# Four dense layers with paged attention on one core: six weight loads dropped, 64 small subtractions moved from VectorE to GpSimd

## The chip, the core and the metric

The kernel runs on one core of one Trainium2 chip. The core has TensorE (PE) for matrix products, VectorE (DVE), ScalarE (ACT) and GpSimd (POOL) for everything else, and SyncE (SP), which here only issues transfers; 16 DMA engines move data between the device memory and the on-chip memory. The engines run their own instruction streams, each strictly in order, and meet through semaphores. The metric is the device time of one execution in microseconds; the kernel is run several times and the median is taken. Separately one execution is recorded by the hardware profiler; times inside the kernel come from that one.

## The reference

An input `x` of 64 sequences of 32 rows with 512 features (2048 rows) goes through four residual layers, `x = x + ffn(cond(x))`:

- Layer 0: one of 8 weight matrices per sequence, then a two-matrix ReLU² network plus a routed low-rank part, and a layer norm.
- Layer 1: a gated network (512 to 1376 and back) with a low-rank update per sequence, then a 512x512 product with a thresholded mixture of low-rank experts.
- Layer 2: paged attention, 32 query heads over 8 key and value heads of width 128, against 512 cached keys per sequence (16 pages of 32 rows, named by a table of indices) and the 32 new rows, with a norm and a rotation on queries and keys, and an output product by `Wo` (4096 to 512); then a 512x512 product with 2 of 8 low-rank experts.
- Layer 3: one of 32 small mixing matrices per sequence, a 512x512 product, and low-rank updates.

All of it is float32.

## The kernel before

The 2048 rows are 16 tiles of 128 rows (`NT`), each of four sequences. The layers run one after the other; layer 3 and the dense part of layer 2 form a common tail.

**Layer 1** (`layer1`) takes two tiles at a time: 8 groups of 256 rows. For a group, `features(f)` for f = 0 to 10 forms the gate and up products for one chunk of 128 of the 1376 features; each ends in two DVE instructions (L426, L427) that write a slice of `actT`. `down` then accumulates the product with the down weights in four blocks `pz`. Its last part (chunk 10 and the low-rank term, L438) needs `low_d`, which `low_down` computes with small PE products and one DVE instruction (`masked`, L384). The main loop (L512) interleaves the groups: beside the products of group g come the choice of experts and the output of group g-1 and the loads for group g+1 (`load_updates`: the first halves `A` of the low-rank updates by SP, and three gathers `Bg`, `Bu`, `Bd` by POOL; `load_x`: two tiles `xt`).

Layer 1 also prepares something for layer 2. The output product of layer 2 multiplies two-by-two blocks of matrices with 7 instead of 8 products, for which four sums of blocks of `Wo` are wanted. `sum_up` (L272) makes three steps for one block row: `rows` loads two pieces of 256 KB (L283, SP), `add` forms four differences of 128x256 (L289 to L292), `store` writes 512 KB to the device memory (L295, SP). There are 16 such sums, two per group. Loaded and computed tiles come from one ring of three buffers named `sum`, so the load for sum k+2 needs the buffer that the store of sum k reads. The tile framework orders instructions of independent work by priority, and it brings the sums forward: the program has nearly all 16 inside the first of the 8 groups, ahead of instructions of `low_d` on DVE.

**Layer 2** (`attention`) goes through 32 steps: two halves of the heads (`HALVES`), for each the 16 tiles. In step s, PE works on the scores and values of tile s, and between them, at fixed places called slots, on the projections of step s+1 (values, keys and four groups of query heads, with 4 matmuls of 512 columns per pair of places) and on the output product of earlier tiles. A step has 32 slots; which work stands at which slot is written out by hand (`plan`, `then`, `slots`, L1056 to L1121). Every projection weight tile (`wv`, `wk`, and four `wq`, 1 MB each) has one buffer, holding the weights of the current half. The weights of the second half are loaded over those of the first by this part:

```
if steps[s + 2][0] != h:
    for what, at in zip(("v", "k") + GROUPS, (4, 6, 9, 12, 15, 18)):
        slots[at].append(partial(weights, steps[s + 2][0], what))
```

Here `h` is the half of step s. The condition holds for s = 14 and for s = 15. In step 14 each load stands after the last use of the weights by the projections of step 15, which is the last of the first half. In step 15 the same six loads stand once more. An odd step's plan has the keys at slots 2 and 4, the query groups at 5 and 6, 8 and 9, 11 and 13, 19 and 20, and the values at 22 and 24, so the loads of step 15 come after the projections of step 16 for keys and query groups 0 to 2, and before those for query group 3 (load at slot 18) and for the values (load at slot 4).

SP issues all of these loads and also the page loads `kt` in one queue in program order.

Of the kernel before, what the change touches and what calls it, by code (L numbers as in the profile page):

```python
# [28 lines left out]
ALU = mybir.AluOpType  # L29
# [242 lines left out]
def sum_up(c, pool, sums, h, k):  # L272


    nc, a = c.nc, c.a
    H = D // 2
    w, t = [], []

    def rows():
        w.append(pool.tile([P, 4, H], F32, name="sum", bufs=3))  # L280
        for n in range(2):
            at = (h * HQP + n * HQP // 2 + k) * HD
            nc.sync.dma_start(w[0][:, 2 * n:2 * n + 2, :].rearrange("p a b -> p (a b)"),  # L283
                              a["WoT"][at:at + HD, :])

    def add():
        t.append(pool.tile([P, 4, H], F32, name="sum", bufs=3))
        (b11, b12, b21, b22), (t1, t2, t3, t4) = ([v[0][:, n, :] for n in range(4)] for v in (w, t))
        nc.vector.tensor_tensor(t1, b12, b11, ALU.subtract)  # L289
        nc.vector.tensor_tensor(t3, b22, b12, ALU.subtract)  # L290
        nc.vector.tensor_tensor(t2, b22, t1, ALU.subtract)
        nc.vector.tensor_tensor(t4, b21, t2, ALU.subtract)  # L292

    def store():
        nc.sync.dma_start(sums[h][:, k], t[0])  # L295

    return rows, add, store
# [340 lines left out]
def attention(c, known, x_in, y_part, y_out, sums, tail):  # L638
# [14 lines left out]
    tc, nc, a = c.tc, c.nc, c.a  # L653
    half = HD // 2
    n_c = L // P
    with ExitStack() as outer:
# [304 lines left out]
        steps = [(h, T) for h in range(HALVES) for T in range(NT)]  # L961
# [91 lines left out]
        for s, (h, T) in enumerate(steps):  # L1053
# [35 lines left out]
            if s + 2 < len(steps):  # L1089
                slots[18].append(projections[s + 2].load)  # L1090
                slots[24].append(projections[s + 2].tables)
                slots[29 if s < 2 else 26].append(projections[s + 2].x)
                if steps[s + 2][0] != h:

                    for what, at in zip(("v", "k") + GROUPS, (4, 6, 9, 12, 15, 18)):
                        slots[at].append(partial(weights, steps[s + 2][0], what))
# [268 lines left out]
def emit(tc, a, layers=(0, 1, 2)):  # L1365
    with ExitStack() as ctx:
        c = Common(ctx, tc, a)
        dram = ctx.enter_context(tc.tile_pool(name="scratch", bufs=1, space=DRAM))

        def scratch(name):  # L1370
            tiles = [dram.tile([P, D], F32, name=f"{name}_{t}") for t in range(NT)]
            return lambda t: tiles[t]

        def rows(name):
            return lambda t: a[name][t * P:(t + 1) * P, :]

        x = rows("x")
        for n in layers:
            out = rows("out") if n == layers[-1] else scratch(f"x{n}")
            if n == 0:  # L1380
                layer0(c, x, out)
            if n != 0 and n == next(m for m in layers if m):
                kp = ctx.enter_context(tc.tile_pool(name="known", bufs=1))
                last = Tail(c)
                last.numbers(kp)
                known = Known(c, kp)
                sums = [dram.tile([P, HQP // 2, 4, D // 2], F32, name=f"wo_sums{h}") for h in range(HALVES)]
            if n == 1:
                layer1(c, kp, x, out, sums)
            elif n == 2:  # L1390
                y_part, y = scratch("y_part"), scratch("y")
                attention(c, known, x, y_part, y, sums, last.between(x, y, out))
            x = out
# [86 lines left out]
```

## Time and profile before

| | |
|---|---|
| runs of the kernel | median 3666.28 us of 3 (3663.46 to 3667.42) |
| the profiled execution | 3653.76 us, of it 3652.0 us from first to last instruction (the span) |
| PE busy | 3589.3 us, 98% of the span |
| DVE, ACT, POOL busy | 1909.3, 1294.5, 1371.1 us |
| layer 1 in the trace | about 397 to 1071 us |
| layer 2's attention | about 1072 us to the tail |
| moved by DMA | 533.45 MB |

The span is the profiled execution's own stretch from its first to its last instruction; 1.8 us lie around it. "Idle before" of an instruction is the time in which its engine stood still ahead of it, with the event that ended the wait. Idle time of DVE, ACT or POOL costs nothing as long as PE doesn't wait for them.

### The profile page before, as it was taken

To read this page: it belongs to the slowest core of one execution; us is meant where nothing else is said; L and a number is where in the kernel's file an instruction comes from. 1 tells how busy PE (TensorE), PEld (TensorE's weight loads), DVE (VectorE), ACT (ScalarE), POOL (GpSimd) and SP (SyncE) were. 2 spreads that over 40 slices of the span, in tenths; PEclk is the share of its full clock that TensorE was granted. 3 is DMA by queue.
4 is the path that set the end of the run, shared out by engine and by line. 5 is a ranking of instruction groups with operands and counts; after the bars stand their busy time and mean duration, and the time that the engine had idled before them with its cause. 6 is when DMAs were issued, how large, how long until landed. Compare 5 with 4: busy or idle time off the path is not lost.

```text
span 3652.0 us, 60353 instructions
## 1 busy us (share of the span) xinstructions
PE 3589.3 (98%) x19520; PEld 2669.0 (73%) x19520; DVE 1909.3 (52%) x4996; ACT 1294.5 (35%) x3046; POOL 1371.1 (38%) x1343
## 2 busy tenths in 40 slices
PE   8999999999999999999999999999999999999999
PEld 3444778888867788777877877778777788777855
DVE  5453332222226756666666655566566665666533
ACT  1111111111115544444444444444444444444411
POOL 0112100000025644555445453455554544555232
PEclk9999999999999999999999999999999999999999
DMA  5004541110124555555655577555555565556731
GB/s 211 24 27 167 189 136 44 54 52 31 41 93 126 150 184 179 166 174 152 186 184 153 181 224 228 184 153 181 170 184 172 152 189 172 179 173 200 219 99 62
DMA packets 531083, 533.45 MB, mean 146 GB/s; under 512 B 54258, under 2 KB 441330, under 8 KB 530770
## 3 DMA queue, kind: packets, MB, share of 16 engines
q1 hardware_dynamic: 484050, 377.50, 33.4%
q0 software_dynamic: 44416, 147.88, 12.7%
q10 hardware_dynamic: 2304, 4.20, 0.3%
q8 instruction: 159, 2.61, 0.3%
q14 instruction: 154, 1.26, 0.1%
HBM read 500.01 MB, written 29.36 MB: 145 GB/s over the span
## 4 chain that ended last, share of the span: by engine, by line
PE 91%; DVE 4%; DMA 2%; SPq 1%; issue 1%; ACT 1%; POOL 0%; DVEq 0%; ACTq 0%; POOLq 0%
PE po L689 14%; PE sc L900 12%; PE pq L689 12%; PE gate_up L342 10%; PE py L689 9%; PE prT_ps L684 6%; PE pz L342 4%; PE po L1249 3%; PE pv L689 3%; PE pk L689 3%; PE ph L124 3%; PE pd L249 2%; DVE own_vt L722 2%; PE po L342 2%; PE qkT_ps L684 2%; PE py L204 1%
## 5 line engine op out<-in xcount | busy, mean ns | idle before, releaser
L715 POOL DMA_INDIRECT vt<-in_v_rows,v_rows x512 | 499.9, 976 | 592.1 <-PE po L689 486.7
L907 ACT ACTIVATE pr<-pr,low 128x544 f32<-128x544 f32 x512 | 383.4, 749 | 726.9 <-DVE low L905 723.5
L689 PEld LDWEIGHTS po<-prT,vt 128*128 128x128 f32 x4096 | 533.0, 192 | 96.8 <-issue 75.6
L900 PE MATMUL sc<-kt,qT 128*128 128x288 f32 (+1 forms) x2048 | 555.5, 394 | 4.4 <-ACT qT L803 2.4
L689 PE MATMUL po<-prT,vt 128*128 128x128 f32 x4096 | 542.4, 275 | 0.9 <-ACT prT L918 0.9
L905 DVE CUSTOM_DVE_ANT_0 pr<-sc,mask 128x544 f32<-128x544 f32 x512 | 368.8, 720 | 321.6 <-PE sc L900 320.1
L689 PE MATMUL pq<-wq,xT 128*128 128x512 f32 x1024 | 482.3, 594 | 8.3 <-DMA wq<-in_WqT 8.3
L900 PEld LDWEIGHTS sc<-kt,qT 128*128 128x128 f32 x2048 | 370.1, 190 | 154.4 <-issue 64.8
L918 ACT COPY prT<-prT_ps 128x512 f32<-128x512 f32 x512 | 296.0, 578 | 178.8 <-PE prT_ps L684 177.4
L912 DVE TENSOR_SCALAR pr<-pr,low 128x512 f32<-128x512 f32 x512 | 332.8, 650 | 15.2
L684 PE MATMUL prT_ps<-ident,pr 128*128 128x128 f32 x2048 | 311.2, 275 | 0.1
L689 PEld LDWEIGHTS pq<-wq,xT 128*128 128x128 f32 x1024 | 186.2, 191 | 141.7 <-issue 125.8
L909 DVE RECIPROCAL low<-low 128x1 f32<-128x1 f32 x512 | 83.2, 163 | 339.4 <-ACT pr L907 335.5
L684 PEld LDWEIGHTS prT_ps<-ident,pr 128*128 128x128 f32 x2048 | 238.2, 142 | 7.9 <-issue 0.3
L689 PE MATMUL py<-wo,oT 128*128 128x256 f32 x1024 | 241.4, 379 | 0.0
L128 POOL TENSOR_TENSOR rs<-rs,minus_half 128x4 f32<-128x4 f32 x160 | 169.1, 1057 | 160.3 <-DVE rs L731 156.1
L910 ACT ACTIVATE own_pr<-pr,low 128x32 f32<-128x32 f32 x512 | 164.0, 320 | 131.9 <-DVE low L909 130.6
L747 POOL TENSOR_TENSOR rot<-rot,swapped 128x512 f32<-128x512 f32 x160 | 204.9, 1280 | 5.2 <-DVE swapped L744 3.9
L689 PEld LDWEIGHTS py<-wo,oT 128*128 128x128 f32 x1024 | 187.5, 190 | 22.0
L722 DVE COPY own_vt<-v 32x128 f32<-32x128 f32 x512 | 171.6, 335 | 36.7 <-PE po L689 24.7
L689 PE MATMUL py<-wo,o_sum 128*128 128x256 f32 x768 | 181.5, 380 | 0.2
L730 DVE TENSOR_REDUCE rs<-squares 128x4 f32<-128x512 f32 x160 | 109.3, 683 | 136.2 <-ACT squares L728 134.5
(226 smaller groups left out, 5106.3 us busy)
## 6 DMA issues: line engine op xcount, KB each, us to landing
kt<-in_kT SPq DMA_DIRECT2D x2048, 64.0 KB
wo<-wo_sums SPq DMA_DIRECT2D x128, 512.0 KB
wo<-in_WoT SPq DMA_DIRECT2D x96, 512.0 KB
xt<-x SPq DMA_DIRECT2D x48, 256.0 KB
wq<-in_WqT SPq DMA_DIRECT2D x12, 1024.0 KB
A<-in_A SPq DMA_DIRECT2D x64, 152.0 KB
sets<-in_cond0T SPq DMA_DIRECT2D x32, 256.0 KB
sum<-in_WoT SPq DMA_DIRECT2D x32, 256.0 KB
```

The lines of the kernel that those rows point to most:

```text
L128: self.nc.gpsimd.tensor_tensor(t, t, self.minus_half[:, :n], ALU.pow)
L342: c.on_pe(nc.tensor.matmul(out, lhsT, rhs, start=start, stop=stop))
L684: c.on_pe(nc.tensor.transpose(pt[:, m, :], piece, c.ident))
L689: c.on_pe(nc.tensor.matmul(out, lhsT, rhs, start=first and i == 0, stop=last and i == len(pairs) - 1))
L715: nc.gpsimd.indirect_dma_start(out=vts[b % 2][:, n, :], out_offset=None, in_=a["v_rows"], in_offset=bass.IndirectOffsetOnAxis(ap=rows[h][: ...
L722: nc.vector.tensor_copy(own_vts[b % 2][g * S:(g + 1) * S, g % 2, :], v[j * S:(j + 1) * S, g * HD:(g + 1) * HD])
L747: nc.gpsimd.tensor_tensor(r, r, tmp, ALU.add)
L900: c.on_pe(nc.tensor.matmul(sc[:, lo + n * PSIZE:lo + m * PSIZE].rearrange("p (n k) -> p n k", k=PSIZE), q, kt[:, n:m, g, :], start=True, s ...
L905: nc.vector.tensor_tensor_reduce(pr[:, :NK], sc[:, lo:lo + NK], masks[h, b], -SCALE, 3.0e38, ALU.add, ALU.min, low[:, 0:1])
L907: nc.scalar.activation(pr[:, :NK], pr[:, :NK], AF.Exp, bias=low[:, 0:1], scale=-1.0, accum_out=low[:, 1:2])
L912: nc.vector.tensor_scalar(pr[:, :L], pr[:, :L], low[:, 2:3], None, ALU.mult)
L918: nc.scalar.copy(prT, pt)
```

## The change

Two edits that don't touch each other.

```
 def add():                                     # in sum_up
-    nc.vector.tensor_tensor(t1, b12, b11, ALU.subtract)
-    nc.vector.tensor_tensor(t3, b22, b12, ALU.subtract)
-    nc.vector.tensor_tensor(t2, b22, t1, ALU.subtract)
-    nc.vector.tensor_tensor(t4, b21, t2, ALU.subtract)
+    nc.gpsimd.tensor_tensor(t1, b12, b11, ALU.subtract)
+    nc.gpsimd.tensor_tensor(t3, b22, b12, ALU.subtract)
+    nc.gpsimd.tensor_tensor(t2, b22, t1, ALU.subtract)
+    nc.gpsimd.tensor_tensor(t4, b21, t2, ALU.subtract)
...
-    if steps[s + 2][0] != h:                   # in attention
+    if steps[s + 2][0] != steps[s + 1][0]:
         for what, at in zip(("v", "k") + GROUPS, (4, 6, 9, 12, 15, 18)):
             slots[at].append(partial(weights, steps[s + 2][0], what))
```

The first puts the 64 subtractions of layer 1 into POOL's stream. The second makes the condition true only for s = 14, where step s+2 is of another half than step s+1; the six loads of step 15 are no longer issued. The instructions of PE and ACT and their order stay as they were. DVE's order is the old one without the 64 subtractions. On SP the six loads of step 15 are gone, and in layer 1's first group some stores and loads of the sums change places with each other and with the loads of `A`.

## Prediction, made before the changed kernel was run

> **What bounds the kernel now.** I read the page's first part, then the waits of PE, then the two stretches around the two waits that touch the change. PE is busy for 98% of the span:
>
> ```profile
> PE 3589.3 (98%) x19520; PEld 2669.0 (73%) x19520; DVE 1909.3 (52%) x4996; ACT 1294.5 (35%) x3046; POOL 1371.1 (38%) x1343
> ```
>
> So only what PE waits for can be won: 3652.0 - 3589.3 = 62.7 us, the start of the program included. The list of PE's waits (total us, times, longest) has its largest entries here:
>
> ```profile
> PE py L204 <- DVE w L200: 12.1, 2, 11.0
> PE pq L689 <- DMA wq<-in_WqT: 8.3, 1, 8.3
> PE pz L342 <- DVE low_d L384: 6.7, 1, 6.7
> ```
>
> The first is layer 0's start, untouched. The second is one wait for a query weight load, the third one wait in layer 1. PE in time, first around the second entry:
>
> ```profile
> 2245.47 1.18 PE L900 MATMUL sc<-kt,qT 128*128 128x288 f32 x4
> 2255.00 3.57 PE L689 MATMUL pq<-wq,xT 128*128 128x512 f32 x4 [8.35 <-DMA wq<-in_WqT]
> 2258.40 0.60 PE L684 MATMUL qkT_ps<-ident,rot 128*128 128x128 f32 x4
> 2260.17 1.88 PE L689 MATMUL pq<-wq,xT 128*128 128x512 f32 x4
> ```
>
> Besides the 8.35 us of standing still, the four matmuls behind it take 3.57 us, and the same four 1.88 us a little later. SP's queue has the culprit, the last of the step's six repeated loads (start, duration of the issue):
>
> ```profile
> 2245.14 0.43 SPq L100 DMA_DIRECT2D wq<-in_WqT  x1
> ```
>
> Query group 3 is projected at slot 19 of step 15, its reload stands at slot 18, so PE waits for a megabyte that it already had.
>
> The third entry, on DVE in time:
>
> ```profile
> 469.93 0.43 DVE L292 TENSOR_TENSOR sum<-sum 128x256 f32<-128x256 f32 x1
> 474.66 0.43 DVE L289 TENSOR_TENSOR sum<-sum 128x256 f32<-128x256 f32 x1 [4.31 <-DMA sum<-in_WoT]
> 475.00 0.42 DVE L384 TENSOR_TENSOR low_d<-low_d_ps,own 128x256 f32<-128x256 f32 x1
> ```
>
> DVE stands 4.31 us before a subtraction whose block of `Wo` hasn't landed, with `low_d` queued behind it; its PE products were done at about 467.3. Then the same work of PE in group 0 and in group 1 (length, busy time per engine, granted clock, DMA), from the first matmul of `low_d_ps` to the first of the next group:
>
> ```profile
> 465.84:480.76 14.92, 8.25 (x169) 6.72 (x169) 9.23 (x20) 0.59 (x1) 0.00 (x0) 0.77 0.74 231
> 557.16:563.00 5.84, 5.84 (x169) 5.31 (x169) 3.15 (x4) 0.59 (x1) 0.00 (x0) 1.00 0.22 59
> ```
>
> The same 169 matmuls take 14.92 us with sums in DVE's queue and 5.84 us without.
>
> **What the Trainium skill says.** "TensorE: Matmul & The Clock Gate", What's actually happening: after an idle window of about 3.4 us the array runs at half its clock until it has been busy as long. The trace agrees: the clock of 0.77 above, and 3.57 against 1.88 us. "GPSIMD Engine Reference", Performance versus the Vector engine: an add of two float32 operands took 1.96 times as long as on VectorE. Here the nearest rows are POOL's additions of the same shape, L875 at 821 ns and L876 at 724 ns mean, against 424 ns for L289: 1.7 to 1.9. "SBUF — State Buffer", Who interferes with whom: a VectorE instruction with two inputs in SBUF, or a copy in a two-port mode, and a GpSimd instruction lock each other out for the length of one instruction; one with a single SBUF input doesn't contend. The trace agrees: one L292 took 1.43 us beside POOL's 1.27 us addition at 440.09, while L426, which has one PSUM input, took its 0.42 us beside another at 435.33.
>
> **Part 1, the weights.** Removed: six SP issues and 6 MB. From the start of the score matmuls at 2245.47 to the transposes at 2258.40 are 12.93 us. Undisturbed these are 0.92 (four `sc`) + 1.72 (four `pq`), as the chain of waits spaces them elsewhere: 2.64. Gain 12.93 - 2.64 = 10.3 us. What could be late next: nothing that PE waits for in step 13, which has the same plan and no loads (PE busy 75.95 of 76.00 us from 2035 to 2111). DVE was just in time for `sc` at 2245.47 (its L905 ended at 2245.41), so a few tenths may come back. The `xt` and page loads move forward. The first loading, in step 14, stays; PE stood nowhere in it (76.00 of 76.00 us from 2111 to 2187).
>
> **Part 2, the sums.** Removed from DVE: 16 x (424 + 421 + 417 + 487) ns = 28 us of busy time, worth nothing in itself, and the waits for `Wo` rows with what is queued behind them. Gain on PE: 14.92 - 5.84 = 9.1 us. After that `low_d` starts at about 467.3, ends at 467.7, and PE needs it at about 468.5 as in group 1.
>
> Added to POOL: 64 subtractions. I take 821 ns for the first of each sum and 724 ns for three: 3.0 us a sum, 48 us in all; bounds 0.42 us each (DVE's) and 1.28 us (L747, twice the elements). POOL was busy for 7.2 us in group 0 and has room. Behind them on POOL stand the bias additions to `xt` (used by outputs a group later), `Bg` and `Bu` for group 2 (issued at 446.8 before, about 456 now, used at about 554), and `Bd` (481 before, used at about 630): all free.
>
> The pace of the sums matters through SP. Per pair: subtract, subtract, store, load two blocks again. Undisturbed pairs began at 458.54, 466.35 and 474.66, 8.1 us apart; with 3.0 instead of 1.8 us a sum this is some 10.5. Over the seven gaps from sum 0 to sum 14 that is at most +17; in the stretch where the third group's `A` and index loads already held SP from 477 to 486 it costs less. Walking through the new order of SP I get the last store at about 506 instead of 495.8, at most 513. Behind it stand the output of the first tile and the load of `xt` for group 2 (505.67 before). PE transposes that tile at 525.98, now at 525.98 - 9.1 = 516.9; a load of this size took 3.75 us (470.81 to 474.56), so it must be issued by 513.1. Expected 506 to 507: hidden with 6 us in hand, none at the upper end. Without this cover each us late is a us of PE.
>
> Port lock: DVE's copies of `A` and the small instructions of `choose` can each wait up to 0.8 us for a POOL subtraction. The second group needs `low_x` some 2.4 us after it is ready and `hw` some 6 us after; the gating instructions have one PSUM input. Taken as 0, bounds 0 and +3 us.
>
> **Sum.** 3652.0 - 10.3 - 9.1 = 3632.6 us of span, 3634.4 with the 1.8 us around it, against 3653.76. The median of the runs is 12.5 us above the profiled execution; where those lie isn't shown, so I subtract the same 19.4: 3666.3 - 19.4 = 3646.9 us (-0.53%).
>
> **Rivals.** A: one of the two waits comes back under another name. If DVE, no longer resting in step 15, holds PE at `sc`, or the second group is held by locked copies, only about half is won: 3666.3 - 9.1 = 3657.2 or 3666.3 - 10.3 = 3656.0. For it: DVE is at 83% from 2220 to 2250. Against: step 13 does the same at full PE.
> B: nothing measurable. The waits depend on when transfers land; one execution shows them. If the unrecorded runs don't have them: 3666. Against: the reload at slot 18, one slot before its use, and the order of DVE are fixed in the program. That the reload isn't removed is excluded: the condition is false for s = 15, and the changed program issues six `Wq`, `Wk`, `Wv` loads fewer.
> C, slower: POOL's pace delays SP's `xt` load for group 2. It costs from an issue at 513.1 on; it eats all 19.4 us when the last store comes at about 532, 37 us later than before: 5.2 us per pair, 2.6 per sum, so a sum of 4.4 us, 1.1 us per subtraction. L876 at 0.72 speaks against it; only lock waits at nearly every subtraction would bring it there. Then 3670.
>
> **How the numbers follow.** Both gains whole or nearly (3642 to 3651): 78%. A, with a late `xt` of some us counted in: 13%, 3651 to 3659. B: 5%, 3666. C: 4%, 3668 to 3672. Unrecorded runs may wait longer than the recorded one, so I go 10 us below the likeliest; above, to 3658, which takes in both forms of A. A measurement of this kernel tells some 0.2% (7 us) from no change; chances from the cases: faster 78 + 13 = 91%, same 5%, slower 4%.
>
> **What would show it.** In the profile after: no PE wait on `wq` in step 15 and the 2.6 us between scores and transposes; `low_d` within 1 us of its PE products and a clock of 1.00 there; group 0's tail at 5.8 us; subtractions on POOL of 0.7 to 0.8 us; the last store of the sums at 500 to 513; no PE wait on `xT_ps` near 517; 527.2 MB moved. Wrong if PE waits newly on `xt`, `sc` or `low_x`, or if POOL needs over 1 us each.

## The result, and the profile after

The changed kernel takes 3648.71 us (median of 5 runs, 3642.11 to 3650.3) against 3666.28 us before (median of 5, 3663.46 to 3672.93). The ratio is 0.9947 with a 95% interval of 0.9933 to 0.9962: faster by 17.6 us. Forecast were 3646.9 us and a gain of 19.4.

The first recorded execution of the changed kernel has a span of 3646.9 us, only 5.1 us under the 3652.0 of before, while the runs differ by 17.6. So the two records must not be subtracted as a whole; stage by stage they say more. The page's first part, and PE's waits with the longest totals:

```profile
PE 3589.7 (98%) x19520; PEld 2665.6 (73%) x19520; DVE 1894.8 (52%) x4932; ACT 1296.2 (36%) x3046; POOL 1415.8 (39%) x1407
```

```profile
PE py L204 <- DVE w L200: 12.0, 2, 10.6
PE po L689 <- ACT prT L918: 6.3, 8, 1.7
PE ph L124 <- DVE z L262: 4.5, 2, 3.7
```

Neither the wait for `wq` nor the one for `low_d` is in the list any more. In the second place stand eight waits for `prT` (the transposed attention weights) in the attention stage; in the record of before there were two, 0.9 us in all.

Step 15 on PE in time, from the score matmuls to the transposes:

```profile
2246.61 1.18 PE L900 MATMUL sc<-kt,qT 128*128 128x288 f32 x4
2247.64 1.88 PE L689 MATMUL pq<-wq,xT 128*128 128x512 f32 x4
2249.35 0.60 PE L684 MATMUL qkT_ps<-ident,rot 128*128 128x128 f32 x4
```

2.74 us where there were 12.93: 10.2 us less, and the four projections run at the full clock.

The same 169 matmuls of group 0's tail (length, busy times of PE, weight loads, DVE, ACT, POOL, granted clock, DMA), and `low_d` on DVE:

```profile
464.61:470.44 5.83, 5.83 (x169) 5.30 (x169) 3.15 (x4) 0.58 (x1) 3.28 (x5) 1.00 0.53 183
```

```profile
466.11 0.42 DVE L384 TENSOR_TENSOR low_d<-low_d_ps,own 128x256 f32<-128x256 f32 x1 [17.39 <-PE low_d_ps L342]
```

5.83 us where there were 14.92: 9.1 us less. `low_d` now waits for its products and for nothing else, and POOL's 3.28 us of subtractions beside it don't show on PE.

Where the rest went can be seen because PE executes the same 19520 matmuls in the same order in both kernels, so that the start of each can be set against the start of its counterpart, with the first matmul as zero. My reckoning, after minus before (us):

```
stage of the program                        first record of after   second record of after
before group 0's tail (468 us)                       -0.9                  -1.6
after group 0's tail                                -10.0                 -10.6
start of step 15's wait (2245 us)                    +1.4                 -10.2
after it                                             -8.7                 -20.3
last matmul                                          -4.6                 -19.4
```

Both gains are there in full in both records. In between, the first one loses 11 us in the attention stage, most of it in steps of 0.4 to 1.9 us, and 4 more after step 15. The second loses 0.4 and 0.9 us in these two places. Experiment 4 asks whose these losses are.

### The profile page after: what moved, and what is told of

Read it like the earlier page. It is cut to its first block, busy times and chain, and to the rows that moved or that the text cites. A ratio compares the mean times of both kernels' runs of the same rounds, so it can differ in the third digit from the quotient of the medians.

```text
span 3646.9 us, 60352 instructions
## 1 busy us (share of the span) xinstructions
PE 3589.7 (98%) x19520; PEld 2665.6 (73%) x19520; DVE 1894.8 (52%) x4932; ACT 1296.2 (36%) x3046; POOL 1415.8 (39%) x1407
## 4 chain that ended last, share of the span: by engine, by line
PE 85%; DVE 8%; ACT 2%; DMA 2%; issue 1%; SPq 1%; DVEq 0%; POOL 0%; another core or an unknown queue 0%; ACTq 0%; POOLq 0%
PE po L689 12%; PE sc L900 11%; PE gate_up L342 10%; PE pq L689 9%; PE py L689 9%; PE prT_ps L684 5%; PE pz L342 5%; PE po L1249 3%; PE ph L124 3%; PE pk L689 3%; PE pv L689 3%; PE pd L249 2%; DVE own_vt L722 2%; PE po L342 2%; DVE pr L905 1%; PE qkT_ps L684 1%
## 5 line engine op out<-in xcount | busy, mean ns | idle before, releaser
L912 DVE TENSOR_SCALAR pr<-pr,low 128x512 f32<-128x512 f32 x512 | 341.1, 666 | 15.1
L426 DVE TENSOR_TENSOR sg<-sg,gate_up 128x256 f32<-128x256 f32 (+1 forms) x88 | 37.0, 421 | 276.0 <-ACT sg L425 276.0
```

The source lines that it names most:

```text
L912: nc.vector.tensor_scalar(pr[:, :L], pr[:, :L], low[:, 2:3], None, ALU.mult)
```

## The experiments

Every ratio is to runs of the kernel before on the same chip, on the same occasion; its median there is given, since the level moved between occasions. The ratios are formed from all the runs and not from the two medians; they differ from the quotient of the medians by up to 0.0005. Line numbers are those of the kernel that was run, so they are shifted by a few in experiment 3.

### 1. Each edit alone

The weights alone, the kernel before with

```
-                if steps[s + 2][0] != h:
+                if steps[s + 2][0] != steps[s + 1][0]:
```

> The kernel before with the condition on the weight loads alone changed; the sums stay on VectorE. Theory of the prediction: the two waits are independent, so this takes 10.3 us: 3656 us, ratio 0.997; in the profile no wait on wq in step 15, and still about 6.7 us of PE waiting for low_d in group 0. Rival (the whole gain of the medians comes from this edit, the sums being hidden anyway): 3649 us. Rival (the gain of the medians is a drift of the attention stage between executions, not the edits): any time between 3640 and 3670 with both waits as predicted, the rest moved in layer 2.

Measured: 3642.92 us against 3656.15, ratio 0.9969 [0.9957, 0.9982]. The sums alone, the kernel before with the four lines

```
-        nc.vector.tensor_tensor(t1, b12, b11, ALU.subtract)
+        nc.gpsimd.tensor_tensor(t1, b12, b11, ALU.subtract)
...
```

> The kernel before with the four subtractions alone moved to GpSimd; the weights are still loaded twice. Theory: takes 9.1 us: 3657 us, ratio 0.9975; no wait on low_d, group 0's tail at 5.8 to 5.9 us, and the wait on wq in step 15 still 8 to 9 us. Rival (the sums are hidden anyway): 3666 us. If the gains add, e1 and e2 together give the 17.6 us of the medians within a few us.

Measured: 3645.52 us against 3656.15, ratio 0.9972 [0.9963, 0.9982]. PE's waits, first with the weights alone, then with the sums alone:

```profile
PE pz L342 <- DVE low_d L384: 7.6, 1, 7.6
```

```profile
PE pq L689 <- DMA wq<-in_WqT: 11.5, 1, 11.5
```

Each edit takes away its own wait and leaves the other's. The times lie 11 to 13 us under the expected ones, as the kernel before is 10 us lower on this occasion; the ratios are close to those expected. The two ratios miss 1 by 0.0031 and 0.0028, together 0.0059; both edits at once miss it by 0.0053, and on later occasions by 0.0061 and 0.0058. The gains add within the intervals, and the rivals in which one edit is the whole gain are out.

### 2. Which of the six loads, and what it waits for

The kernel before without the last repeated load, and with only that one:

```
 for what, at in zip(("v", "k") + GROUPS, (4, 6, 9, 12, 15, 18)):
+    if even or what != HKP - 1:      # five reloads; "what == HKP - 1" for the last alone
         slots[at].append(partial(weights, steps[s + 2][0], what))
```

> The kernel before without the last of the six repeated loads (query group 3); five megabytes are still loaded again, and the sums stay on VectorE. Theory (the reload one slot ahead of its use costs, not the traffic): no PE wait on wq, ratio 0.997 as with the whole condition changed. Rival (the traffic of all six delays pages and other weights): half of the gain at most, ratio 0.9985 or more, with PE waiting on kt or wo in step 15.

Measured: ratio 0.9972 [0.9962, 0.9982] (3649.59 against 3660.8), and PE waits for no `wq`:

```profile
2246.78 1.18 PE L900 MATMUL sc<-kt,qT 128*128 128x288 f32 x4
2247.80 1.88 PE L689 MATMUL pq<-wq,xT 128*128 128x512 f32 x4
2249.52 0.60 PE L684 MATMUL qkT_ps<-ident,rot 128*128 128x128 f32 x4
```

That is the gain of the whole edit (0.9969 in experiment 1), and the stretch is at 2.74 us, with five of the six megabytes still moved. Without the last load the five others cost nothing that shows.

> The kernel before with only the last of the six repeated loads kept (query group 3), the sums on VectorE. Theory: PE still waits for that megabyte, but it no longer shares the DMA engines with the five others: a megabyte at 300 to 400 GB/s takes about 3 us[...], so PE waits 3 to 5 us instead of 8 to 11, and 4 to 8 us of 10.3 are left with the slow clock: ratio 0.998 to 1.0. Rival (the queue ahead doesn't matter, only the slot): the wait stays at 8 us or more, ratio 1.0.

Measured: ratio 0.9991 [0.9982, 0.9999] (3658.27 against 3660.8). PE and then SP's queue in time:

```profile
2257.83 3.61 PE L689 MATMUL pq<-wq,xT 128*128 128x512 f32 x4 [6.49 <-DMA wq<-in_WqT]
```

```profile
2246.21 3.03 SPq L100 DMA_DIRECT2D wo<-in_WoT  x2
2249.30 0.50 SPq L100 DMA_DIRECT2D wq<-in_WqT  x1
2251.36 10.64 SPq L100 DMA_DIRECT2D kt<-in_kT  x14
```

The wait is 6.5 us, between what the two theories gave: my 3 to 5 us were too low. Without the five others PE still gets the megabyte only 8.5 us after its issue. Two output weight tiles of 512 KB were issued in the 3 us before it and page loads follow, and the DMA engines moved 283 GB/s from the first of these to PE's start; that these transfers make it slow is likely, but no run took them away. With the five others ahead the wait was 8.3 to 11.5 us in four records, so they add 2 to 5 us to it. From the score matmuls to the transposes are 2.7 us without the last load, 11.1 with it alone, and 12.9 to 16.2 with all six: the larger part is this one load's place.

### 3. What the sums cost on VectorE, and what hides them on GpSimd

First the sums on VectorE without anything to wait for (the ring of three buffers becomes one for the block and two for the sums; that part of the edit isn't shown here):

```
 def rows():
+    if kept:
+        w.append(kept[0])
+        return
     ...
+    kept.append(w[0])
...
-    nc.sync.dma_start(sums[h][:, k], t[0])
+    nc.sync.dma_start(sums[h][:, k], w[0])
```

> The changed weight condition, and the 64 subtractions on VectorE again, but without anything to wait for: one block of Wo is loaded once, all 16 sums are formed from it, and the stores send that block (so the loads of 15 blocks and the use of the sums are left out, and layer 2 multiplies with other numbers). All 64 subtractions stand ahead of low_d, where before it were 49. Theory (the wait in VectorE's queue cost the 9.1 us, not VectorE's work): group 0's tail 5.9 us, low_d within 1 us of its products, ratio 0.994 as the changed kernel. Rival (the 28 us of VectorE work cost it): low_d still late by some us, ratio 0.997 as with the weights alone.

Measured: ratio 0.9948 [0.9932, 0.9965] (3639.79 against 3660.8), the gain of both edits. Group 0's tail, with the columns as above:

```profile
463.05:468.90 5.85, 5.85 (x169) 5.07 (x168) 3.15 (x4) 0.59 (x1) 0.00 (x0) 1.00 0.14 37
```

All 64 subtractions stand ahead of `low_d` on VectorE, their work is unchanged, and PE doesn't wait: they are over at 439 us, before `low_d` is wanted. So the amount of VectorE's work was not the cause; what had put that work off until `low_d` was wanted were the waits for `Wo` rows. This kernel also moves less by DMA at that time (37 GB/s in this stretch, 231 before), which this run alone can't tell apart from the missing waits. The kernel with the sums alone on GpSimd (experiment 1) can, as it keeps all the loads:

```profile
464.25:470.10 5.85, 5.85 (x170) 5.32 (x170) 3.15 (x4) 0.58 (x1) 2.60 (x4) 1.00 0.63 223
```

At 223 GB/s its tail is as short. Neither the work nor the traffic held PE, but waiting for rows in the queue in which `low_d` stood.

Then the cover of the sums on GpSimd, the changed kernel with each subtraction done twice:

```
+        for _ in range(2):
             nc.gpsimd.tensor_tensor(t1, b12, b11, ALU.subtract)
             ...
```

> The changed kernel with every one of the 64 subtractions done twice on GpSimd: nothing else. Theory (rival C of the prediction: the sums are free only as long as SP's queue gets past their last store in time): a sum takes 5.8 instead of 2.9 us, a pair 5.8 more, over seven pairs the last store comes at some 540 to 547 instead of 507, and the load of xt behind it lands after 516, when PE wants to transpose it: PE waits 28 to 34 us for xT_ps, ratio to before 1.001 to 1.004. Rival (GpSimd has room, so doubling its work is free too): ratio as the changed kernel's, 0.994.

Measured: ratio 1.0036 [1.0022, 1.0051] (3673.77 against 3660.8), slower than before with both waits gone. SP's queue and PE in time:

```profile
540.87 0.33 SPq L296 DMA_DIRECT2D wo_sums<-sum  x1
541.29 0.38 SPq L493 DMA_DIRECT2D x<-o  x1
541.72 0.78 SPq L85 DMA_DIRECT2D xt<-x  x1
```

```profile
545.48 1.12 PE L378 MATMUL xT_ps<-ident,xt 128*128 128x128 f32 x4 [30.68 <-DMA xt<-x]
```

The last store comes at 540.87 and the two `xt` loads wait behind it; PE stands 30.7 us. The same three rows of the changed kernel:

```profile
506.78 0.33 SPq L295 DMA_DIRECT2D wo_sums<-sum  x1
507.19 0.38 SPq L492 DMA_DIRECT2D x<-o  x1
507.63 0.78 SPq L85 DMA_DIRECT2D xt<-x  x1
```

```profile
515.66 0.60 PE L377 MATMUL xT_ps<-ident,xt 128*128 128x128 f32 x4
```

From issue to use are 3.76 us in the doubled kernel (545.48 - 541.72). So the change had 515.66 - 507.63 - 3.76 = 4.3 us in hand. Rival C is a real mechanism; by this reckoning it starts 4.3 us beyond where the change lies.

### 4. The time given back in the attention stage

Both kernels unaltered, recorded again.

> The kernel before, unaltered, recorded once more. The first recorded execution was 12.5 us under the median of the runs, so its 3652.0 us are not typical. If that lies in the attention stage, a second record has both waits as before (8 to 9 and 6 to 7 us) and is longer than the first by up to 12 us, spread over many waits of 0.5 to 2 us in layer 2. If it lies in the two waits instead, these are longer in this record, up to 20 us together more.

Measured: ratio 1.0000 [0.9992, 1.0008] (3655.34 us), span of the record 3656.4. Both waits as before (10.1 and 5.9 us). The record is only 4.4 us longer than the first and has only one of the many short losses expected: 4.1 us more arise just before step 15's wait (2150 to 2244 us), 2.0 more in that wait, and 1.8 less ahead of group 0's tail. So this record didn't decide where the 12.5 us lie.

> The changed kernel, unaltered, recorded once more. Theory: both waits absent, group 0's tail 5.9 us, times 3642 to 3651. The first record gave back 14.6 us in layer 2 against the first record of before. If that belongs to the change, this record shows the same steps of about 0.5 us at the same places; if it is the execution, the places and the sum differ, by 5 us or more.

Measured: ratio 0.9939 [0.9926, 0.9953] (3634.01 against 3656.15), span of the record 3632.3 us: 19.7 us under the first record of before, and 0.3 us from the 3632.6 that the prediction had for it. The times lie 8 us under the expected range, since on this occasion the level is lower. The waits of the attention stage in it are much as before, with `prT` at 0.2 us. Then once more on another occasion, on the same chip:

> The changed kernel, unaltered, a third record, beside a third record of the kernel before on the same chip. Ratio 0.994. The time given back in layer 2 (14.6 us in the first record of it, 0 in the second) belongs to the chip: here either both this record and that of the kernel before show the waits of 0.5 to 2 us in the attention stage, or neither does.

> The kernel before, unaltered, a third record. Ratio 1.0. If the waits in the attention stage belong to the change and not to the chip, this record has none of them while that of the changed kernel on the same chip has.

Measured: 3644.11 against 3666.22, ratio 0.9942 [0.9928, 0.9956], and 3665.64, ratio 0.9999 [0.9991, 1.0007]. The changed kernel's third record has the losses again, with eight waits for `prT` between 1090 and 3400 us, 5.5 us in all. PE's waits in the same stretch in the third record of the kernel before:

```profile
PE pq L689 <- DMA wq<-in_WqT: 9.8, 1, 9.8
PE po L689 <- ACT prT L918: 3.8, 9, 1.7
```

The kernel before now shows the waits for `prT` that the first record of the changed kernel had; in its own first record they came to 0.2 us in this stretch. By the same setting of matmul against matmul, this record ends 13.4 us later than the first of the same kernel; 9.5 of them are 16 steps of 0.4 to 1.8 us from one matmul to the next (those over 0.3 us) in the attention stage, 14 of them at places where the first record of the changed kernel has one too. The other records agree: the four of the occasion of experiment 1 have two such steps at most, and the seven of the two later occasions, on two chips, have 11 to 16 each, whichever kernel it is. The losses belong to the occasion and not to the kernel; the two first records must then come from unlike occasions (inferred, not shown). That would also explain the 12.5 us between the first record of before (3653.76) and its runs (3666.28). What makes them is not settled: most of them sit where the products of the new values end and the output is copied (`own_part`), and no run changed anything there. The eight records with the losses also hold about 9% fewer semaphore events than the five others (57,000 to 57,400 against 62,800 to 62,900); whether the two have one cause isn't known.

### 5. One weight load later

In six of the ten records up to here PE waits 1.1 to 2.5 us about the end of step 14 for an output weight tile (`wo`) issued among the weights of the first loading; in the other four it doesn't wait there. The changed kernel with the values' load moved into step 15:

```
-                if steps[s + 2][0] != steps[s + 1][0]:
+                if steps[s + 2][0] != h:
...
+                        if (what == "v") != even:
                             slots[at].append(partial(weights, steps[s + 2][0], what))
```

> The changed kernel with the value weights of the second half loaded in step 15 (slot 4, used at slot 22) instead of step 14; the other five stay in step 14, each still loaded once. In step 14 PE waits some 1.3 to 2.2 us in the records for an output weight tile queued behind these loads. Theory: a megabyte less there takes that wait away, 1 to 2 us, too little for the runs to tell: ratio as the changed kernel's, 0.994, and the record shows no wait on wo in step 14. Rival: the load of step 15 delays something there, PE waits on wo, kt or wv around slot 22, ratio 0.995 or more.

Measured: ratio 0.9936 [0.9922, 0.9949] (3643.3 against 3666.22) beside 0.9942 [0.9928, 0.9956] for the changed kernel on the same occasion; the wait in step 14 is 0.7 us. The unaltered changed kernel recorded on the same occasion has none there at all, so the record doesn't show that the later load took anything away, and the times can't be told apart. It is no proven improvement.

## Why the prediction was right, step by step

- **Part 1, 10.3 us.** Right: 10.2 in the first record (12.93 to 2.74), and the start of step 15 against its end moves by 10.1 in the first and the second. Of the "few tenths" that might come back, 0.1 did (2.74 for 2.64). One thing the working left open, whether the five other loads share the blame, is answered by experiment 2: alone they cost nothing that shows, ahead of the sixth they lengthen its wait.
- **Part 2, 9.1 us.** Right, 14.92 to 5.83, and in every record without VectorE's wait. `low_d` began 0.25 us after the last of its small products was issued (466.11 against 465.86 for the next group of matmuls).
- **The price of a subtraction.** 724 ns was right for all four (means 724 to 734); the 821 ns for the first of each sum was not needed. A sum is 2.9 us, not 3.0.
- **The pace of the sums.** The last store was put at about 506, at most 513: 506.78. In hand were put 6 us: 4.3, as `xt` was issued at 507.63 and PE came at 515.66, 1.2 us earlier than the 516.9 reckoned, 0.9 of it since the record is ahead by that much already before group 0's tail.
- **The port lock, taken as 0.** Nothing of it shows on PE: group 0's tail has a clock of 1.00 and PE busy throughout, and PE waits for nothing in the group after it. On VectorE it does show: beside POOL's subtractions at 483.8 to 486.7, three small instructions of `choose` (L465, L466, L472) took 0.81, 0.65 and 0.58 us for 0.29, 0.17 and 0.23 before. L466 has a single input, so the prediction's "one with a single SBUF input doesn't contend" was too wide.
- **The sum.** 3632.6 us of span were forecast from the record of before. The second record has 3632.3, the first 3646.9. The forecast took the 12.5 us between record and runs as something that both kernels share, without knowing where; it was the right choice for the median (19.4 forecast, 17.6 measured on the first occasion, 22.1 on the second and third) but the step "where those lie isn't shown" was the gap in the working. Experiment 4 shows that the level belongs to the occasion and that most of the difference lies in the attention stage; that this holds for these 12.5 us too is inferred.
- **Luck in the sizes.** Both parts were read from one record of before, and each of them varies. With all six loads the stretch of step 15 takes 14.6 to 16.2 us in the three other records, which makes part 1 worth 11.9 to 13.5 us; with the waits on VectorE group 0's tail takes 14.1 to 15.6 us in five others, so part 2 is 8.3 to 9.8. And the time of 3646.9 us held for the level of the first occasion: on the second the changed kernel took 3634.01.
- **The rivals.** A (half the gain) and B (nothing) didn't occur. C, the slower one, was placed well: doubling the work gave a wait of 30.7 us for 28 to 34 forecast before that run, and a ratio over 1. Its stated point of decision, 1.1 us per subtraction, was not reached at 0.73; at twice 0.73 it was.

## What to carry to other kernels

An engine's share of busy time says nothing of what an instruction costs in its queue: 28 us of subtractions, on an engine busy for a quarter of layer 1, cost PE nothing that showed as work, and 9.1 us where they waited for transfers with an instruction behind them that PE needed. Move the waiting, not the work; and before moving it, follow the wait onto the new engine and through the queue that serves it, here SP's, for the distance to the next use, which was 4.3 us. A repeated load is harmless or costly mainly by its place: five of the six cost nothing by themselves, and the sixth, one slot ahead of its use, made PE wait 6.5 us alone and 8.3 to 11.5 us with the five ahead of it.

Two records of one kernel differed by 13 us here, as much as either edit gained. Set the stages against each other, and record both kernels twice, before explaining a loss that only one pair shows.

## What was unexpected of the hardware

The same program, unaltered, had records of 3652.0, 3656.4 and 3665.0 us on different occasions with the clock at 0.995 to 0.996 in all. Of the 13 us between the first and the last, 9.5 lay in 16 steps of 0.4 to 1.8 us in the attention stage, and six of these points have such a step in all eight records with losses, of seven different kernels. And a megabyte issued behind two half megabytes reached PE 8.5 us after its issue, at 283 GB/s of total traffic.
